# Edge attention on one core: score clipping and exponentials for two batches at a time, ScalarE's address reads behind its copies, norms one round later, 191 column tiles

## The chip, the cores and the metric

The kernel runs on one core of one Trainium2 chip. Its metric is device time in microseconds; the number that counts is the median of several executions. A profile is one further execution, recorded by the hardware profiler. Engines go by the profile's names: PE is TensorE (PEld its weight load), DVE VectorE, ACT ScalarE, POOL GpSimd, SP SyncE.

## The reference, cut to what matters

One graph attention layer with 6250 nodes and 206250 edges, 128 features in 8 heads of 16, edges sorted by destination:

```python
Qh, Kh, Vh = (h @ WQ), (h @ WK), (h @ WV)            # 6250 x 8 x 16 each
Eh = edge_attr @ WE                                   # 206250 x 8 x 16
score = einsum('ehd,ehd,ehd->eh', Kh[src], Qh[dst], Eh) / 4
score = exp(clip(score, -5, 5))
wV = segment_sum(Vh[src] * score[:, :, None], dst)
Z = segment_sum(score, dst)
out = layernorm(h + wV / (Z + 1e-6))
```

## The kernel before, in words

A **tile** is 128 edges (one per partition); there are 1612. A **batch** is four tiles (the last eight tiles go in smaller ones), 406 batches in all. `edge_attention` first writes a table of K and V rows to HBM, then runs one **round** per batch; the loop at L626 writes down the order of the instructions of every engine by hand. For a batch b the work is spread over three rounds:

- Round b (`stage_a`): PE multiplies the edge attributes by WE (`eps`, L498) and expands the destination's Q rows by a transposed one-hot (`qps`, L501).
- Round b+1 (`stage_b`): DVE multiplies K by Q (`kq`, L508), by the edge product (`kqe`, L511), sums over each head (`sc`, L514) and clips the scores to -20..20 (L517). At the round's end ACT (`weigh`) takes the exponential twice, into the message tile `msg` (L524) and into PSUM, `exp_p` (L525), a single buffer.
- Round b+2: DVE multiplies V by `exp_p` (`messages`, L558) and PE adds the batch into its window of 128 nodes with a one-hot (`stage_c`, `agg`, L578). One-hots are built for two batches at a time (`together`, L470 and L483), so every second round has two more DVE instructions.

K and V rows of a tile's sources reach SBUF in one of two ways. Most tiles are **gathered**: POOL issues one indirect DMA per tile (L430) from the table. POOL's queue holds little else, so it runs ahead of the rounds by as many batches as the 12 `kvrows` buffers and a manual dependency allow. One tile in some batches is a **column tile**: its sources' columns are copied out of the resident x by ACT (80 copies of one column, L403) and DVE (24 instructions that take two columns each, L400), PE multiplies the tile by the K and V weights (`colkv`, L412), and ACT puts the result into `kvrows` (L419). `COLP = (13, 6)` means six column tiles in 13 batches, 176 in all. The copies come in runs (ACT 10 runs of 8 a tile, DVE 6 runs of 4 instructions), spread over the rounds by `columns`. Before a run, the engine reads the run's column addresses from SBUF into registers (L392, one `TENSOR_LOAD` a run); `columns` reads for the next run before it issues the copies of this one. ACT's runs stand at two places of a round: behind the two exponentials, and at the start of the next round.

When all windows of two node blocks are there (24 times, about every 16 rounds), `finish` has PE add them up (`finps`, L537), ACT copies the result at the end of the round (`fin`, L551), and a layer norm of some 22 small DVE steps starts in the next round, first with `rz` (L791). `fill` issues one such step, or one of the Q rows that the next batches need, at each of four places in a round.

Of the kernel before, what the change touches and what calls it, by code (L numbers as in the profile page):

```python
# [9 lines left out]
F32 = mybir.dt.float32  # L10
# [17 lines left out]
MW = D + H  # L28
CH = 8
GB = 12  # L30
XB = 12
# [5 lines left out]
LAST = NT - TAIL  # L37
# [12 lines left out]
QLOOK = 3  # L50
QREG = 16
COL0 = 24
COLP = (13, 6)
COLA = (8, 10)
COLV = (8, 6)
COLL = 8
RING = 4096
XCOLS = 5
SUMS = 9
XT_AT = RING + P  # L60
NB = (N + P - 1) // P

# [40 lines left out]
def edge_attention(ctx: ExitStack, tc: tile.TileContext, x, xT, srcT, srcC, dstT, dstB, dst0, bnd, lo, eaT,  # L103
                   wq, wkv, we, out, kv, qtab, qs, relD):
    nc = tc.nc
# [35 lines left out]
    with ExitStack() as fast:  # L141
# [99 lines left out]
        wp = fast.enter_context(tc.tile_pool(name="work", bufs=3))  # L241
# [55 lines left out]
        xbs, stores, norms, pending, ready, finished, loaded_x = {}, [], [], [], [], [], set()  # L297
# [47 lines left out]
        chunks, aggs, sums, st8, expanded = {}, {}, {}, {}, {}  # L345

        def load_chunk(c):
            if c in chunks or c * CH >= NT:
# [21 lines left out]
        addresses, fetched = {}, {}  # L370

        def columns(eng, b, share=1.0, most=99):

            size, runs = COLA if eng is nc.scalar else COLV
            first = 0 if eng is nc.scalar else COLA[0] * COLA[1]
            engine = mybir.EngineType.Activation if eng is nc.scalar else mybir.EngineType.DVE
            copy = eng.copy if eng is nc.scalar else eng.tensor_copy
            due = int((b - COL0 + COLL - 1 + share) * runs * COLP[1] / COLP[0] + 1e-6)
            total = len(col_batches) * runs
            while copied.get(engine, 0) < min(due, total) and most:  # L380
                most -= 1
                k, j = divmod(copied.get(engine, 0), runs)
                copied[engine] = copied.get(engine, 0) + 1
                if k not in col_tiles:
                    col_tiles[k] = wp.tile([P, P], F32, name="xcol", bufs=XCOLS)
                to, j = col_tiles[k].bitcast(U8), first + j * size
                known = addresses.setdefault(engine, [])
                while len(known) < 2 and fetched.get(engine, 0) < total:
                    kf, jf = divmod(fetched.get(engine, 0), runs)
                    fetched[engine] = fetched.get(engine, 0) + 1  # L390
                    jf = first + jf * size
                    known.append(nc.values_load_multi_w_load_instructions(  # L392
                        col_at[kf % col_half:kf % col_half + 1, kf // col_half, jf:jf + size], engines=(engine,),
                        min_val=XT_AT, max_val=XT_AT + 8 * (N - 1) + 4,
                        skip_runtime_bounds_check_because="edges name nodes")[1])
                at = known.pop(0)
                if eng is nc.vector:
                    for c in range(0, size, 2):
                        both = [xT_bytes[:, ds(a - XT_AT, 8)] for a in at[c:c + 2]]
                        eng.tensor_tensor(to[:, 4 * (j + c):4 * (j + c) + 8], *both, op=ALU.bitwise_or)  # L400
                    continue
                for c in range(size):
                    copy(to[:, 4 * (j + c):4 * (j + c) + 4], xT_bytes[:, ds(at[c] - XT_AT, 4)])  # L403

        def project_columns(b):

# [47 lines left out]

        def together(b):

            t0 = batches[b][0]
            n = len(batches[b])
            if n == B and b + 1 < nbat and len(batches[b + 1]) == B and t0 % (2 * B) == 0:
                return [b, b + 1]  # L460
            return [] if n == B and t0 % (2 * B) else [b]

        def stage_0(b):
            group = together(b)
# [40 lines left out]
        def stage_b(b):  # L505
            n, g, oh, pq, pe = st8[b]
            t0 = wp.tile([P, B, D], F32, name="kq", bufs=2)
            nc.vector.tensor_tensor(t0[:, :n], g[:, :n, :D], pq[:, :n], op=ALU.mult)  # L508
# [4 lines left out]
            sc = wp.tile([P, B, H], F32, name="sc")  # L513
            nc.vector.tensor_reduce(sc[:, :n], t1[:, :n].rearrange("p b (h d) -> p b h d", h=H),  # L514
                                    axis=AX.X, op=ALU.add)
            yield
            nc.vector.tensor_scalar(sc[:, :n], sc[:, :n], -20.0, 20.0, op0=ALU.max, op1=ALU.min)  # L517
            st8[b] = [n, g, oh, sc]

        def weigh(b):  # L520

            n, g, oh, sc = st8[b]
            m = wp.tile([P, B, MW], F32, name="msg")
            nc.scalar.activation(m[:, :n, D:], sc[:, :n], AF.Exp, scale=0.25)  # L524
            nc.scalar.activation(exp_p[:, :n], sc[:, :n], AF.Exp, scale=0.25)  # L525
            st8[b] = [n, g, oh, m]

        def windows(q):

# [24 lines left out]
            blocks_out.append(copied_out)  # L554

        def messages(b):
            n, g, oh, m = st8[b]
            nc.vector.tensor_tensor(  # L558
                m[:, :n, :D].rearrange("p b (h d) -> p b h d", h=H),
                g[:, :n, D:].rearrange("p b (h d) -> p b h d", h=H),  # L560
                exp_p[:, :n, :, None].to_broadcast([P, n, H, DH]), op=ALU.mult)

        def stage_c(b):
            n, g, oh, m = st8.pop(b)
            for i in range(n):
                t = batches[b][i]
                k, _ = window_of(t)
                q = t * N // NT // P
                if q % 2 == 0 and q < NB and q not in loaded_x:
                    loaded_x.add(q)  # L570
                    xbs[q] = load_x(nc, sp, x, q, min(2, NB - q))
                final = k == NT
                if k not in aggs:
                    aggs[k] = psA.tile([P, 1, MW], F32, name="agg")
                    if final:
                        add_windows(aggs[k][:, 0], QL, True, False)
                tail = t == NT - 1 or window_of(t + 1)[0] != k
                nc.tensor.matmul(aggs[k][:, 0], oh[0][:, oh[1] + i * P:oh[1] + i * P + P], m[:, i, :],  # L578
                                 start=not final and t % (QUAD * G) == 0, stop=tail)
                if tail and final:  # L580
                    norms.insert(0, layernorm(nc, sp, aggs.pop(k), xbs.pop(QL), out, QL, 1, stores))
                elif tail:
                    sums[k] = sp.tile([P, MW], F32, name="sum", bufs=SUMS)
                    nc.scalar.copy(sums[k], aggs.pop(k)[:, 0])
# [40 lines left out]
        held, late = [], []  # L625
        for b in range(nbat + 3):  # L626
            if b >= XB and not manual:
                manual.append(fast.enter_context(tc.manual_schedule()))
# [4 lines left out]
            if b < nbat:  # L633
# [3 lines left out]
                g = gathered.pop(b)  # L637
# [221 lines left out]
```

## Time and profile before

| | |
|---|---|
| median of 3 runs | 1847.12 us (1847.1 to 1848.22) |
| profiled execution, its own time | 1840.47 us |
| its span | 1838.7 us |
| mean granted TensorE clock | 0.931 |
| PE / DVE / ACT / POOL busy | 71% / 94% / 87% / 75% |
| gathers issued by POOL | 1436 |
| clips, exponentials | 406, 812 |

The profile lists groups of instructions with their count, busy time and mean duration, then the time that the engine stood idle before them and what ended it. Small instructions overlap at their ends, so the start of the next one, in the timeline, tells better than the duration what one costs its engine. "issue" as the reason for a wait means that nothing in the profile held the engine: it was its own sequencer, for instance while it read addresses into registers (shown as ACTq and DVEq).

### The profile page before, as it was taken

To read this page: it belongs to the slowest core of one execution; us is meant where nothing else is said; L and a number is where in the kernel's file an instruction comes from. 1 tells how busy PE (TensorE), PEld (TensorE's weight loads), DVE (VectorE), ACT (ScalarE), POOL (GpSimd) and SP (SyncE) were. 2 spreads that over 40 slices of the span, in tenths; PEclk is the share of its full clock that TensorE was granted. 3 is DMA by queue.
4 is the path that set the end of the run, shared out by engine and by line. 5 is a ranking of instruction groups with operands and counts; after the bars stand their busy time and mean duration, and the time that the engine had idled before them with its cause. 6 is when DMAs were issued, how large, how long until landed. Compare 5 with 4: busy or idle time off the path is not lost.

```text
span 1838.7 us, 48927 instructions
## 1 busy us (share of the span) xinstructions
PE 1299.2 (71%) x9130; PEld 1118.7 (61%) x9130; DVE 1720.6 (94%) x7478; ACT 1608.3 (87%) x15268; POOL 1375.8 (75%) x1443
## 2 busy tenths in 40 slices
PE   6886667676676777776777667766767667766776
PEld 4776656565665666665666556655656656655665
DVE  5579999999999999999999999999999999999998
ACT  2339889899999999999999999999999999999994
POOL 6777777777777777777777777777777777777774
PEclk8999899889989899999899999999999999899989
DMA  8776667676776577677667766866876676667762
GB/s 281 231 228 199 192 183 225 194 205 196 211 221 202 177 224 216 182 208 221 202 199 213 226 192 183 241 198 180 241 213 191 192 229 194 203 185 232 217 191 77
DMA packets 170631, 376.74 MB, mean 205 GB/s; under 512 B 58423, under 2 KB 84369, under 8 KB 170315
## 3 DMA queue, kind: packets, MB, share of 16 engines
q0 software_dynamic: 68144, 185.10, 35.0%
q1 hardware_dynamic: 101031, 187.38, 33.9%
q14 instruction: 242, 1.98, 0.3%
q8 instruction: 74, 1.21, 0.3%
q10 hardware_dynamic: 1140, 1.06, 0.2%
HBM read 358.60 MB, written 14.81 MB: 203 GB/s over the span
## 4 chain that ended last, share of the span: by engine, by line
DVE 42%; DMA 17%; ACT 13%; PE 11%; issue 6%; DVEq 5%; POOL 4%; ACTq 2%; SPq 0%; POOLq 0%
DMA kvrows<-kv,src 14%; ACT xcol L403 11%; DVE xcol L400 8%; DVE kqe L511 6%; DVE kq L508 6%; DVE sc L514 6%; POOL kvrows L430 4%; DVEq L392 4%; DVE onehot L470 4%; PE eps L498 4%; DVE msg L558 4%; PE agg L578 3%; DVE onehotT L483 2%; ACTq L392 2%; DMA dB_sb<-dstB 1%
## 5 line engine op out<-in xcount | busy, mean ns | idle before, releaser
L430 POOL DMA_INDIRECT kvrows<-kv,src x1388 | 1328.6, 957 | 423.0 <-issue 313.0
L403 ACT COPY xcol<-xT_sb 128x4 uint8 x14080 | 1422.3, 191 | 60.5 <-issue 54.2
L498 PE MATMUL eps<-we_sb,ea 128*128 128x128 f32 x3224 | 488.9, 298 | 384.8 <-issue 182.7
L498 PEld LDWEIGHTS eps<-we_sb,ea 128*128 128x128 f32 x3224 | 425.0, 205 | 482.6 <-issue 353.7
L578 PE MATMUL agg<-msg,onehot 128*128 128x136 f32 x3224 | 526.0, 310 | 109.4 <-DVE msg L558 101.1
L578 PEld LDWEIGHTS agg<-msg,onehot 128*128 128x128 f32 x3224 | 447.0, 208 | 165.6 <-DVE msg L558 152.2
L400 DVE TENSOR_TENSOR xcol<-xT_sb 128x8 uint8 x4224 | 416.1, 156 | 8.7 <-issue 4.6
L508 DVE TENSOR_TENSOR kq<-kvrows,qps 128x512 f32<-128x512 f32 x406 | 274.0, 675 | 35.2 <-PE qps L501 17.1
L558 DVE TENSOR_TENSOR msg<-kvrows,exp_p 128x512 f32<-128x512 f32 x406 | 271.1, 668 | 7.5 <-ACT exp_p L525 7.5
L511 DVE TENSOR_TENSOR kqe<-kq,eps 128x512 f32<-128x512 f32 x406 | 272.3, 671 | 3.1 <-PE eps L498 2.6
L514 DVE TENSOR_REDUCE sc<-kqe 128x32 f32<-128x512 f32 x406 | 270.2, 665 | 0.5
L501 PE MATMUL qps<-qw,onehotT 126*128 126x128 bf16 x1612 | 166.6, 227 | 0.0
L524 ACT ACTIVATE msg<-sc 128x32 f32<-128x32 f32 x406 | 92.6, 228 | 72.0 <-DVE sc L517 64.5
L470 DVE TENSOR_TENSOR onehot<-iota_p,dst_sb 128x512 f32<-128x512 f32 (+2 forms) x206 | 137.5, 668 | 2.0 <-PE agg L578 2.0
L501 PEld LDWEIGHTS <-onehotT 126*128 126x128 bf16 x1612 | 132.9, 102 | 8.2
L412 PE MATMUL colkv<-wkv_sb,xcol 128*128 128x256 f32 x352 | 114.2, 409 | 0.8 <-ACT xcol L403 0.8
L483 DVE TENSOR_SCALAR onehotT<-relb,node 126x1024 bf16<-126x1024 bf16 (+2 forms) x206 | 100.0, 486 | 3.3 <-DMA relb<-relD 2.0
L517 DVE TENSOR_SCALAR sc<-sc 128x32 f32<-128x32 f32 x406 | 82.1, 202 | 0.3
L525 ACT ACTIVATE exp_p<-sc 128x32 f32<-128x32 f32 x406 | 73.7, 182 | 0.0
L419 ACT COPY kvrows<-colkv 128x256 f32<-128x256 f32 x176 | 63.8, 362 | 0.3 <-PE colkv L412 0.3
L430 POOL DMA_INDIRECT kvrows<-x,src x48 | 46.3, 964 | 22.5 <-issue 11.6
L412 PEld LDWEIGHTS colkv<-wkv_sb,xcol 128*128 128x128 f32 x352 | 59.7, 209 | 1.0 <-ACT xcol L403 1.0
(76 smaller groups left out, 537.3 us busy)
## 6 DMA issues: line engine op xcount, KB each, us to landing
ea<-eaT SPq DMA_DIRECT2D x201, 512.0 KB
relb<-relD SPq DMA_DIRECT2D x100, 504.0 KB
kvrows<-kv,src POOLq DMA_INDIRECT x1388
qw<-qs SPq DMA_DIRECT2D x202, 31.5 KB
kv<-kvst SPq DMA_DIRECT2D x12, 512.0 KB
qs<-qst SPq DMA_DIRECT2D x48, 96.0 KB
xst<-xT SPq DMA_DIRECT2D x12, 256.0 KB
xb<-x SPq DMA_DIRECT2D x24, 128.0 KB
```

The source lines that it names most:

```text
L400: eng.tensor_tensor(to[:, 4 * (j + c):4 * (j + c) + 8], *both, op=ALU.bitwise_or)
L403: copy(to[:, 4 * (j + c):4 * (j + c) + 4], xT_bytes[:, ds(at[c] - XT_AT, 4)])
L412: nc.tensor.matmul(pk, col_tiles.pop(k), wkv_sb, start=True, stop=True)
L430: ins = nc.gpsimd.indirect_dma_start(out=g[:k, i, :f], out_offset=None, in_=rows, in_offset=bass.IndirectOffsetOnAxis(ap=src_col(t)[:k], a ...
L470: nc.vector.tensor_tensor(tl[:, HW:].rearrange("p (t n) -> p t n", n=P)[:, :n, :HW], iota_p[:, None, :].to_broadcast([P, n, HW]), rel[:, t ...
L498: nc.tensor.matmul(pe[:, i, :], ea[:, i * P:i * P + P], we_sb, start=True, stop=True)
L501: expanded[b] = nc.tensor.matmul(pq[:, i, :], ohT[:, i * P:i * P + P], loaded[t0 // WT], start=True, stop=True)
L508: nc.vector.tensor_tensor(t0[:, :n], g[:, :n, :D], pq[:, :n], op=ALU.mult)
L511: nc.vector.tensor_tensor(t1[:, :n], t0[:, :n], pe[:, :n], op=ALU.mult)
L514: nc.vector.tensor_reduce(sc[:, :n], t1[:, :n].rearrange("p b (h d) -> p b h d", h=H), axis=AX.X, op=ALU.add)
L558: nc.vector.tensor_tensor(m[:, :n, :D].rearrange("p b (h d) -> p b h d", h=H), g[:, :n, D:].rearrange("p b (h d) -> p b h d", h=H), exp_p[ ...
L578: nc.tensor.matmul(aggs[k][:, 0], oh[0][:, oh[1] + i * P:oh[1] + i * P + P], m[:, i, :], start=not final and t % (QUAD * G) == 0, stop=tail)
```

## The change

Four edits, and sizes that follow from them:

- **Pairs.** Batches 12 to 399 are clipped and weighed in pairs (2i, 2i+1). Both write their head sums into one tile `sc` of eight tiles' width; behind the second one DVE clips all 64 columns at once, and ACT takes the two exponentials of 64 columns at once. `sc`, `msg` and `exp_p` are twice as wide; `sc` and `msg` have two buffers, not three. Messages and aggregation of both batches move one round later, to b+3, one batch in each round as before. Batches 0 to 11 and from 400 on go alone, at their old places. `kvrows` of a paired batch is held one round longer, with the same 12 buffers.
- **Address reads.** ACT reads the addresses of its next run behind the copies of a run, one run ahead. DVE's reads stay in front, two runs ahead.
- **Norms.** A layer norm starts one round later (`waiting`), but not in the last rounds.
- **Column tiles.** `COLP` is (2, 1): one column tile in every two batches, 191 in all, so 15 more, with 15 fewer gathers. `XCOLS` goes from 5 to 4 buffers of a column tile, `SUMS` from 9 to 8.
- `together` now also pairs the small last batches, which makes two one-hot builds fewer there.

```diff
-COLP = (13, 6)
+COLP = (2, 1)
-XCOLS = 5
-SUMS = 9
+XCOLS = 4
+SUMS = 8
...
-        exp_p = psX.tile([P, B, H], F32, name="exp_p")
+        exp_p = psX.tile([P, 2 * B, H], F32, name="exp_p")
...
-                while len(known) < 2 and fetched.get(engine, 0) < total:
...
+                fetch(2 if eng is nc.vector else 1)
                 at = known.pop(0)
...
                     copy(to[:, 4 * (j + c):4 * (j + c) + 4], xT_bytes[:, ds(at[c] - XT_AT, 4)])
+                fetch(1)
...
+        def group_of(b):
+
+            if b < XB or b >= LAST // B - 1:
+                return [b]
+            return [b - b % 2, b - b % 2 + 1]
+
+        def weighed(r):
+
+            return [b for b in (r - 3, r - 2) if 0 <= b < nbat and b + (3 if len(group_of(b)) > 1 else 2) == r]
...
-            nc.vector.tensor_scalar(sc[:, :n], sc[:, :n], -20.0, 20.0, op0=ALU.max, op1=ALU.min)
-            st8[b] = [n, g, oh, sc]
+            if b == group[-1]:
+                nc.vector.tensor_scalar(sc[:, :k + n], sc[:, :k + n], -20.0, 20.0, op0=ALU.max, op1=ALU.min)
...
-            n, g, oh, sc = st8[b]
-            m = wp.tile([P, B, MW], F32, name="msg")
+            group = group_of(b)
+            if b != group[-1]:
+                return
+            sc, n = scores.pop(group[0]), sum(len(batches[i]) for i in group)
+            m = wp.tile([P, 2 * B, MW], F32, name="msg", bufs=2)
...
-            norms.extend(pending)
+            norms.extend(waiting)
+            waiting[:] = pending
             pending.clear()
+            if b >= nbat - 3:
+                norms.extend(waiting)
+                waiting.clear()
...
-            if 0 <= b - 2 < nbat:
-                messages(b - 2)
+            for i in weighed(b):
+                messages(i)
...
-            if 0 <= b - 2 < nbat:
-                stage_c(b - 2)
+            for i in weighed(b):
+                stage_c(i)
```

How this moves instructions. First ACT, in the middle of the program, where a round's exponentials stand (`xcol` is the column tile being filled, `col_at` the table of addresses, `kvrows<-colkv` the finished column tile's copy). Before:

```order
L403 COPY xcol<-xT_sb 128x4 x8
L419 COPY kvrows<-colkv 128x256
L524 ACTIVATE msg<-sc 128x4x8
L525 ACTIVATE exp_p<-sc 128x32
L392 TENSOR_LOAD col_at
L403 COPY xcol<-xT_sb 128x4 x8
L392 TENSOR_LOAD col_at
```

After, at the end of a pair's second round:

```order
L407 COPY xcol<-xT_sb 128x4 x8
L394 TENSOR_LOAD col_at
L545 ACTIVATE msg<-sc 128x8x8
L546 ACTIVATE exp_p<-sc 128x64
L407 COPY xcol<-xT_sb 128x4 x8
L394 TENSOR_LOAD col_at
```

The read that stood between the exponentials and the next run of copies now stands ahead of the exponentials, behind the run before; between two runs there is one read as before. The next pair of exponentials comes two rounds later, with ten runs between.

Second DVE, from the head sums of one round to the `kqe` product of the next, in the middle of the program. Before (here with no step of a norm):

```order
L514 TENSOR_REDUCE sc<-kqe 128x32
L558 TENSOR_TENSOR msg<-kvrows,exp_p 128x4x128
L392 TENSOR_LOAD col_at
L400 TENSOR_TENSOR xcol<-xT_sb 128x8 x4
L517 TENSOR_SCALAR sc<-sc 128x32
L508 TENSOR_TENSOR kq<-kvrows,qps 128x512
L392 TENSOR_LOAD col_at
L400 TENSOR_TENSOR xcol<-xT_sb 128x8 x4
L511 TENSOR_TENSOR kqe<-kq,eps 128x512
```

After, at the end of a pair's second round; the next round here starts a norm (`rz`):

```order
L531 TENSOR_REDUCE sc<-kqe 128x32
L580 TENSOR_TENSOR msg<-kvrows,exp_p 128x4x128
L394 TENSOR_LOAD col_at
L404 TENSOR_TENSOR xcol<-xT_sb 128x8 x4
L536 TENSOR_SCALAR sc<-sc 128x64
L522 TENSOR_TENSOR kq<-kvrows,qps 128x512
L394 TENSOR_LOAD col_at
L404 TENSOR_TENSOR xcol<-xT_sb 128x8 x4
L817 TENSOR_SCALAR rz<-fin 128x16
L525 TENSOR_TENSOR kqe<-kq,eps 128x512
```

The clip is there in every second round only, at twice the width, and a norm's first step keeps its place in a round but comes a round after the one that copies `fin`. In the whole program DVE has 212 clips for 406, and ACT 1910 runs of copies for 1760.

More of the change, by code (lines that the diff above doesn't have):

```diff
@@ L343, in load_rel @@
                               .to_broadcast([QROWS, n]))
-        chunks, aggs, sums, st8, expanded = {}, {}, {}, {}, {}
+        chunks, aggs, sums, st8, expanded, scores = {}, {}, {}, {}, {}, {}
         def load_chunk(c):
@@ L387, in columns, with fetch @@
                 known = addresses.setdefault(engine, [])
-                while len(known) < 2 and fetched.get(engine, 0) < total:
[L389 to L395, printed above, removed]
+                def fetch(ahead):
+                    while len(known) < ahead and fetched.get(engine, 0) < total:
+                        kf, jf = divmod(fetched.get(engine, 0), runs)
+                        fetched[engine] = fetched.get(engine, 0) + 1
+                        jf = first + jf * size
+                        known.append(nc.values_load_multi_w_load_instructions(
+                            col_at[kf % col_half:kf % col_half + 1, kf // col_half, jf:jf + size],
+                            engines=(engine,), min_val=XT_AT, max_val=XT_AT + 8 * (N - 1) + 4,
+                            skip_runtime_bounds_check_because="edges name nodes")[1])
+                fetch(2 if eng is nc.vector else 1)
                 at = known.pop(0)
@@ L455, in together @@
         def together(b):
[L457 to L461, printed above, removed]
+            first = LAST // B
+            if (b - first if b >= first else b) % 2:
+                return []
+            return [i for i in (b, b + 1) if i < nbat and (i < first) == (b < first)]
+        def group_of(b):
[4 more added lines that the diff above has]
+            return [b for b in (r - 3, r - 2) if 0 <= b < nbat and b + (3 if len(group_of(b)) > 1 else 2) == r]
         def stage_0(b):
@@ L512, in stage_b @@
             yield
[L513 to L514 removed]
+            group = group_of(b)
+            if b == group[0]:
+                scores[b] = wp.tile([P, 2 * B, H], F32, name="sc", bufs=2)
+            sc, k = scores[group[0]], sum(len(batches[i]) for i in group if i < b)
+            nc.vector.tensor_reduce(sc[:, k:k + n], t1[:, :n].rearrange("p b (h d) -> p b h d", h=H),
                                     axis=AX.X, op=ALU.add)
+            st8[b] = [n, g, oh, k]
             yield
[L517 to L518 removed]
+            if b == group[-1]:
+                nc.vector.tensor_scalar(sc[:, :k + n], sc[:, :k + n], -20.0, 20.0, op0=ALU.max, op1=ALU.min)
         def weigh(b):
[L522 to L523 removed]
+            group = group_of(b)
+            if b != group[-1]:
+                return
+            sc, n = scores.pop(group[0]), sum(len(batches[i]) for i in group)
+            m = wp.tile([P, 2 * B, MW], F32, name="msg", bufs=2)
             nc.scalar.activation(m[:, :n, D:], sc[:, :n], AF.Exp, scale=0.25)
             nc.scalar.activation(exp_p[:, :n], sc[:, :n], AF.Exp, scale=0.25)
[L526 removed]
+            for i in group:
+                st8[i].append(m)
         def windows(q):
@@ L623, in fill @@
                 norms.pop(0)
-        held, late = [], []
+        held, late, waiting = [], [], []
         for b in range(nbat + 3):
```

10 lines of the change are left out of this document (5 added, 5 removed).

## The prediction

> **What bounds the kernel now.** The page first: how busy the engines are, and whether that changes over the span.
>
> ```profile
> span 1838.7 us, 48927 instructions
> ...
> PE 1299.2 (71%) x9130; PEld 1118.7 (61%) x9130; DVE 1720.6 (94%) x7478; ACT 1608.3 (87%) x15268; POOL 1375.8 (75%) x1443
> ...
> DVE  5579999999999999999999999999999999999998
> ACT  2339889899999999999999999999999999999994
> POOL 6777777777777777777777777777777777777774
> ```
>
> After two slices of preparation nothing changes: DVE and ACT above 0.8 or 0.9, POOL flat at 0.7. A flat 0.7 is suspicious, so the second view is POOL's own waits.
>
> ```profile
> POOL kvrows L430 <- issue: 324.6, 1065, 0.3
> ...
> POOL kvrows L430 <- PE kvacc L279: 7.2, 3, 6.0
> ```
>
> POOL's longest wait for its sequencer is 0.3 us, 1065 times, and nothing else holds it except in the preparation. A gather is 0.96 us plus a fixed gap of 0.30: POOL issues without a break, and its 75% is full. So I compare paces. The same 400 us in two window tables, gathers (L430) first, then `kq` (L508), one a batch:
>
> ```profile
> 500.00:900.00 400.00, 303.09 (x319) 0.92 0.70 205
> ```
>
> ```profile
> 500.00:900.00 400.00, 61.77 (x92) 0.92 0.70 205
> ```
>
> POOL: 400/319 = 1.254 us a gather, and a batch has 4 - 6/13 = 3.54 of them: **4.44 us a batch**. DVE: 400/92 = **4.35**. POOL began far ahead and DVE gains 0.09 us a batch on it; who waits in the end is in DVE's waits:
>
> ```profile
> DVE kq L508 <- PE qps L501: 17.1, 29, 1.0
> DVE rz L791 <- ACT fin L551: 15.7, 16, 2.5
> ...
> DVE msg L558 <- ACT exp_p L525: 7.5, 10, 1.3
> ...
> DVE kq L508 <- DMA kvrows<-kv,src: 6.5, 6, 1.8
> ```
>
> Only 6.5 us in six waits are for gathered rows, all behind 1377 us. DVE thus sets the pace to about 1400 us and POOL barely the rest: the two limits lie within 7 us of each other. ACT is the third:
>
> ```profile
> ACT msg L524 <- DVE sc L517: 64.5, 75, 4.5
> ACT xcol L403 <- issue: 54.2, 188, 1.2
> ...
> ACT fin L551 <- PE finps L537: 12.3, 10, 2.4
> ```
>
> In 331 of 406 rounds ACT reaches the exponentials after the clip is done, without waiting. It has 131 us of slack in all, 7%.
>
> **The change, part by part.** I sum along DVE, from one batch to the next, against the profiled execution's own 1840.47 us (span 1838.7 and 1.8 around it). The median of the runs shown is 6.65 above that, and I add the difference to it.
>
> *Column tiles, DVE.* The timeline of DVE:
>
> ```profile
> 908.94 0.38 DVE L400 TENSOR_TENSOR xcol<-xT_sb 128x8 uint8 x4
> 909.25 0.14 DVE L809 SCALAR_TENSOR_TENSOR y<-w,y 128x2 f32<-128x2 f32 x1
> 909.32 0.28 DVE L517 TENSOR_SCALAR sc<-sc 128x32 f32<-128x32 f32 x1
> 909.43 0.18 DVE L807 TENSOR_TENSOR w<-y 128x2 f32<-128x2 f32 x1
> ```
>
> A run of four instructions takes 0.31 us from its start to the next one's. 15 tiles x 6 runs x 0.31 = **+27.9 us**. DVE has no idle time to hide them in.
>
> *Column tiles, POOL.* 15 gathers x 1.254 = 18.8 us less issue, and 4.39 us a batch. DVE keeps its distance longer, so its 6.5 us of waits for rows should go: **-6.5**, and no more, since POOL was not the limit before that.
>
> *Clips.* 406 become 212. One costs 0.11 us above (909.32 to 909.43), and 0.08 in front of a large one:
>
> ```profile
> 1792.54 0.17 DVE L517 TENSOR_SCALAR sc<-sc 128x32 f32<-128x32 f32 x1
> 1792.62 0.68 DVE L508 TENSOR_TENSOR kq<-kvrows,qps 128x512 f32<-128x512 f32 x1
> ...
> 1795.03 0.67 DVE L558 TENSOR_TENSOR msg<-kvrows,exp_p 128x512 f32<-128x512 f32 x1
> ```
>
> Width costs little: 8 to 16 columns is 3 ns by the rows of the last batches.
>
> ```profile
> L517 DVE TENSOR_SCALAR sc<-sc 128x16 f32<-128x16 f32 x3 | 0.5, 167 | 0.0
> ...
> L517 DVE TENSOR_SCALAR sc<-sc 128x8 f32<-128x8 f32 x2 | 0.3, 164 | 0.0
> ```
>
> The wide clip is not in the trace; I take 0.02 us more (3 ns x 4 gives 0.01; a second clip's 0.11 is the other end). 194 x (0.09 - 0.02) = **-13.6 us**, between 0 and -19.
>
> *Norms.* `rz` stands second in DVE's queue behind `kq`, with `kqe`, the sums and the messages behind it, and it waits until ACT has copied `fin`, which waits for 16 matmuls. A round later the copy is long there: up to -15.7. But those matmuls also delay PE's next `eps` and `qps`, and what is late next is `kq`. The timeline has the longest but one:
>
> ```profile
> 537.23 3.23 PE L537 MATMUL finps<-sum,shift 128*128 128x136 f32 x16
> ...
> 540.91 0.17 DVE L791 TENSOR_SCALAR rz<-fin 128x16 f32<-128x16 f32 x1 [2.33 <-ACT fin L551]
> ```
>
> With `finps` at 3.23 us, PE comes to the next `eps` that much later, and I expect half of such a wait to return. I take **-11**, between -4 and -15.7.
>
> *ACT.* It gets 15 x 80 more copies, 15 more `kvrows` copies, half the exponentials, and loses the 0.3 us gaps where a read stood bare.
>
> ```profile
> 906.17 4.11 ACT L403 COPY xcol<-xT_sb 128x4 uint8 x40 [0.32 <-issue]
> 910.19 0.23 ACT L524 ACTIVATE msg<-sc 128x32 f32<-128x32 f32 x1
> 910.32 0.18 ACT L525 ACTIVATE exp_p<-sc 128x32 f32<-128x32 f32 x1
> 910.44 3.66 ACT L403 COPY xcol<-xT_sb 128x4 uint8 x37
> ```
>
> Two exponentials take 0.25 us (910.19 to 910.44), the pair's perhaps 0.30. 40 copies take 4.02 us (906.17 to 910.19), 37 start within 3.66: 80 copies are 7.7 to 8.0 us. Two rows more:
>
> ```profile
> 901.13 0.36 ACT L419 COPY kvrows<-colkv 128x256 f32<-128x256 f32 x1
> 901.39 0.23 ACT L524 ACTIVATE msg<-sc 128x32 f32<-128x32 f32 x1
> ```
>
> The `kvrows` copy is 0.26. Sums and `fin` follow from their groups:
>
> ```profile
> L584 ACT COPY sum<-agg 128x136 f32<-128x136 f32 x101 | 26.6, 263 | 4.2 <-PE agg L578 4.0
> ...
> L551 ACT COPY fin<-finps 128x272 f32<-128x272 f32 x24 | 9.2, 384 | 12.6 <-PE finps L537 12.3
> ```
>
> (26.6 + 9.2)/203 pairs is 0.18, less their overlap some 0.13. So ACT needs **8.4 to 8.7 us for a pair**, about 8.55. DVE's pair is 2 x 4.35 = 8.70 now, and after the terms above (1/13 tile x 1.86 = +0.14, clip -0.07, norm -0.06) 8.71. ACT ends up within 2% of DVE. On average it fits, but not pair by pair: a norm adds its 22 steps to about six rounds, and pairs without one are shorter than 8.7. There ACT falls behind. How far it may: from the clip's start to the messages are 2.49 us (1792.54 to 1795.03), of which clip and exponentials take about 0.5; so 2 us, and beyond that `msg` waits on `exp_p`, with `kq` and all else of DVE behind it. I charge **+5 us**, between 0 and +20.
>
> The address read itself:
>
> ```profile
> L392 ACTq TENSOR_LOAD <-col_at x1760: 537/557/1479, 131.5 to 1806.7; - x196
> ```
>
> 0.56 us lie behind eight copies of 0.1. The 40 copies in 4.02 us and the 37 in 3.66 differ by 0.004 us a copy, so some reads are not wholly covered; that is why I take a middle value. The Trainium skill (Advanced Engine Details and Errata, Engine Queue Depths) gives ScalarE a queue of eight instructions, which would cover eight copies' worth, more than 0.56, in every run. By that rule the pair comes to 8.4 and the +5 to about 0; by the 40 copies to 8.7 and to the upper end.
>
> *At nothing.* The 15 `colkv` matmul pairs (PE idles 29%; bare they would be 0.6 us each, 9 in all). The 90 more address reads of DVE, covered by the 1.3 us of reduction and messages ahead (bare 0.6 each). Fewer buffers of `xcol` and `sum`: a column tile is multiplied four rounds after its last copy, and a window is read before its buffer comes round. `kvrows` held a round longer: POOL may run one batch less ahead, 4.4 us, and it loses its lead so slowly now that DVE does not see it. Two fewer one-hots in the tail: at most -0.8.
>
> Sum: 27.9 - 6.5 - 13.6 - 11 + 5 = **+1.8 us, 1842.3 of its own time, 1849 as a median**. The gathers saved are worth 19 us to POOL, but nearly all of it is time that DVE spends on copying columns.
>
> **The rivals.**
>
> 1. *POOL's gain shows.* The looser order takes out most of DVE's waits (`rz`, `msg`, and part of `qps`: 30 to 40 us of 47), and ACT is never late. Then DVE does a pair in 8.6, and the end follows POOL's, which comes 18.8 earlier: -5 to -17, 1830 to 1842. For it: DVE's waits are real and all in rounds that the change loosens. Against: `qps` hangs on PE, which is untouched.
> 2. *ACT becomes the bound.* With 8.7 a pair and `fin`'s 12.3 us of stalls (0.06 a pair), it exceeds DVE's 8.71 from about 8.65 on; `msg` then waits for `exp_p` in most pairs: 0.05 to 0.1 over 190 pairs, on top of +1.8 less the 5: +6 to +16, 1853 to 1863. For it: the 40 copies in 4.02. Against: its stalls shrink when it is late anyway.
> 3. *The norm's wait only moves* to `kq` behind `qps`: +11 more, 1860. Against it: most of the 16 waits are under 1 us, and PE idles.
> 4. *DVE as the one bound.* If only DVE's work counts, columns less clips are +14: 1861. The Trainium skill (Perfetto Trace Analysis, Identifying the Most-Contended Engine) holds that the engine with the highest occupancy is the one to relieve, here DVE at 94%; by it the relief of POOL at 75% is worth nothing. The trace agrees for the first 1400 us, and not for the last 400, where the six waits for rows lie.
>
> **How the numbers follow.** Forecast (-4 to +8, 1843 to 1855): 0.42. Rival 1: 0.28. Rival 2: 0.20. Rivals 3 and 4: 0.05 each. The range leaves out the far end of rival 1 and the last of rival 2: 1834 to 1862. 0.2% of the median is 3.7 us, about what a measurement of this kernel can tell from no change. Faster: rival 1 and 0.04 of the forecast, 0.32. Within: 0.26 of the forecast and 0.01 of the slow ones, 0.27. Slower: 0.41.
>
> **What would show it.** Right: DVE busy up by some 14 us; no waits of `kq` on gathered rows and none of `rz`; ACT near 93%, its waits for issue nearly gone and for the clip fewer; POOL done some 15 us or more before the end with rows waiting; some waits of `msg` on `exp_p` in pairs without a norm. Those waits above 15 us would be rival 2; `kq` on `qps` above 25 us, rival 3; `kq` still waiting for rows with a shorter span, rival 1. Wrong throughout would be a new wait that I have not named, such as gathers held by buffers.

## The result: level, and the profile after

| | before | after |
|---|---|---|
| median (22 executions each, same chip) | 1847.11 us | **1846.78 us** |
| ratio, 95% interval | | 0.9998 [0.9991, 1.0005] |
| profiled execution, its own time | 1840.47 us | 1845.89 us |
| its span | 1838.7 us | 1844.0 us |
| mean granted TensorE clock | 0.931 | 0.923 |

By the medians nothing changed. The two profiled executions differ by 5.4 us, because the one of before lay 6.6 us under its median and the one of after 0.9 us. So the terms are compared from the traces, and the sums from the medians. Of the executions reported below, one of the change without columns (3760.76 us, unexplained) and three of the last group are slow; the ratios leave them out, the medians given do not. First the page of after, engines' busy time:

```profile
span 1844.0 us, 50160 instructions
...
PE 1307.6 (71%) x9160; PEld 1129.0 (61%) x9160; DVE 1731.1 (94%) x7640; ACT 1658.1 (90%) x16095; POOL 1363.4 (74%) x1428
```

DVE has 10.5 us more to do and is still at 94%; POOL has 12.4 us less; ACT went from 87% to 90%. DVE's waits of after (engine and tile, what it waited for, total us, times, longest):

```profile
DVE kq L522 <- PE qps L515: 29.2, 31, 5.0
...
DVE msg L580 <- ACT exp_p L546: 9.0, 11, 1.5
...
DVE kq L522 <- DMA kvrows<-kv,src: 2.5, 2, 1.9
...
DVE rz L817 <- ACT fin L573: 1.9, 1, 1.9
```

The waits for `rz` went from 15.7 to 1.9 us and those for gathered rows from 6.5 to 2.5, while `kq` behind `qps` grew from 17.1 to 29.2 and `msg` from 7.5 to 9.0. These four sum to 4.2 us less. DVE's whole idle time (span less busy time) fell by 5.2 us, so the four hold most of that, and with 10.5 us more work they give +6.3 where the spans differ by 5.3. (That busy and idle time make up the span is so for every engine; what this sum shows is only which waits changed.)

ACT's waits of after:

```profile
ACT msg L545 <- DVE sc L536: 74.0, 71, 7.5
...
ACT fin L573 <- PE finps L559: 8.4, 5, 3.7
...
ACT xcol L407 <- issue: 2.9, 11, 0.6
```

The waits for issue between runs of copies fell from 54.2 us in 188 to 2.9 in 11, which is what ACT gained from reading behind its copies. The same 400 us stretches of after as in the window tables of before, first the gathers (L435):

```profile
500.00:900.00 400.00, 303.41 (x318) 0.95 0.70 207
900.00:1300.00 400.00, 303.41 (x318) 0.94 0.70 207
1300.00:1700.00 400.00, 300.28 (x313) 0.93 0.69 204
```

And `kq` (L522), one a batch:

```profile
500.00:900.00 400.00, 62.45 (x92) 0.95 0.70 207
...
1300.00:1700.00 400.00, 62.41 (x92) 0.93 0.69 204
```

DVE does 92 batches in 400 us, as before. POOL issues 313 instead of 318 gathers in the last stretch: it is now held back, because it stays ahead. POOL's own waits say so:

```profile
POOL kvrows L435 <- issue: 322.8, 1043, 2.1
POOL kvrows L435 <- PE qps L515: 21.1, 41, 4.6
```

And the second of these two lines as it was before:

```profile
POOL kvrows L430 <- PE qps L501: 9.8, 32, 0.3
```

Most of the 41 waits are still the fixed gap of 0.3, but the longest is 4.6: these are gathers that the manual dependency does not let run further ahead. Before, no wait outside the preparation was longer than the fixed gap. Behind the preparation, 15 gathers of after wait 0.5 us or more, 17.4 us beyond the gap. Seven of them (7.4 us, between 255 and 435 us) are of another kind: each starts some 0.74 us behind the end of a `messages` instruction, as a wait for a buffer of `kvrows` would look, and a paired batch keeps that one round longer. It costs nothing here, since POOL is far enough ahead again at 1528 us for the dependency to hold it. At the end of the span the timeline of after has one thing that is not in the trace of before:

```profile
1807.97 2.37 ACT L407 COPY xcol<-xT_sb 128x4 uint8 x24
...
1810.39 1.22 PE L417 MATMUL colkv<-wkv_sb,xcol 128*128 128x256 f32 x2 [5.03 <-ACT xcol L407]
...
1813.78 0.69 DVE L522 TENSOR_TENSOR kq<-kvrows,qps 128x512 f32<-128x512 f32 x1 [5.02 <-PE qps L515]
1814.02 0.94 POOL L435 DMA_INDIRECT kvrows<-kv,src  x1 [4.64 <-PE qps L515]
```

In the brackets: ACT finishes its last column tile late, PE's next instruction waits 5.03 us for it, and `qps`, `kq` and a gather stand behind PE. That is 5.0 of the 12.1 us by which `kq` behind `qps` grew.

### The profile page after: what moved, and what is told of

It reads as the page before. It is cut to its first block, busy times and chain, and to the rows that moved or that the text cites. A ratio compares the mean times of both kernels' runs of the same rounds, so it can differ in the third digit from the quotient of the medians.

```text
span 1844.0 us, 50160 instructions
## 1 busy us (share of the span) xinstructions
PE 1307.6 (71%) x9160; PEld 1129.0 (61%) x9160; DVE 1731.1 (94%) x7640; ACT 1658.1 (90%) x16095; POOL 1363.4 (74%) x1428
## 4 chain that ended last, share of the span: by engine, by line
DVE 41%; PE 19%; ACT 9%; DMA 8%; issue 8%; DVEq 4%; POOL 3%; ACTq 1%; SPq 0%; POOLq 0%
PE agg L600 8%; DVE xcol L404 8%; ACT xcol L407 8%; DMA kvrows<-kv,src 7%; PE eps L512 7%; DVE kqe L525 7%; DVE kq L522 7%; DVE sc L531 5%; DVE msg L580 5%; DVEq L394 4%; DVE onehot L484 3%; POOL kvrows L435 3%; DVE onehotT L497 2%; PE colkv L417 2%; PE qps L515 1%
## 5 line engine op out<-in xcount | busy, mean ns | idle before, releaser
L435 POOL DMA_INDIRECT kvrows<-kv,src x1373 | 1316.8, 959 | 435.9 <-issue 310.1
L407 ACT COPY xcol<-xT_sb 128x4 uint8 x15280 | 1507.6, 192 | 4.4 <-issue 2.9
L404 DVE TENSOR_TENSOR xcol<-xT_sb 128x8 uint8 x4584 | 454.3, 158 | 9.4 <-issue 5.1
L522 DVE TENSOR_TENSOR kq<-kvrows,qps 128x512 f32<-128x512 f32 x406 | 274.2, 675 | 42.3 <-PE qps L515 29.2
L484 DVE TENSOR_TENSOR onehot<-iota_p,dst_sb 128x512 f32<-128x512 f32 (+1 forms) x204 | 137.5, 675 | 0.9 <-PE agg L600 0.9
L417 PE MATMUL colkv<-wkv_sb,xcol 128*128 128x256 f32 x382 | 132.0, 431 | 5.2 <-ACT xcol L407 5.0
L545 ACT ACTIVATE msg<-sc 128x64 f32<-128x64 f32 (+2 forms) x212 | 53.7, 254 | 80.3 <-DVE sc L536 74.0
L497 DVE TENSOR_SCALAR onehotT<-relb,node 126x1024 bf16<-126x1024 bf16 (+1 forms) x204 | 100.4, 492 | 5.3 <-DMA relb<-relD 3.9
L417 PEld LDWEIGHTS colkv<-wkv_sb,xcol 128*128 128x128 f32 x382 | 69.0, 221 | 5.6 <-ACT xcol L407 5.6
L435 POOL DMA_INDIRECT kvrows<-x,src x48 | 45.7, 951 | 22.7 <-issue 12.8
L559 PE MATMUL finps<-sum,shift 128*128 128x136 f32 x370 | 49.4, 287 | 0.0
L536 DVE TENSOR_SCALAR sc<-sc 128x64 f32<-128x64 f32 (+2 forms) x212 | 47.0, 222 | 0.3
```

The source lines that it names most:

```text
L417: nc.tensor.matmul(pk, col_tiles.pop(k), wkv_sb, start=True, stop=True)
L435: ins = nc.gpsimd.indirect_dma_start(out=g[:k, i, :f], out_offset=None, in_=rows, in_offset=bass.IndirectOffsetOnAxis(ap=src_col(t)[:k], a ...
L484: nc.vector.tensor_tensor(tl[:, HW:].rearrange("p (t n) -> p t n", n=P)[:, :n, :HW], iota_p[:, None, :].to_broadcast([P, n, HW]), rel[:, t ...
```

## Experiments

**Theory** (from the prediction and the two traces): there are two limits of nearly one height. One is POOL's 1436 gathers, issued without a break; the other is DVE's queue, with ACT feeding it. The columns relieve POOL and load DVE; pairs, reads and norms relieve DVE; together they cancel. **Rivals**: each edit is worth little anyway (the norm's wait moves to `qps`; reads and pairs are covered), or ACT is what decides. Every kernel was run beside the kernel before on the same chip.

### One edit at a time, on the kernel before

Columns alone:

```diff
-COLP = (13, 6)
+COLP = (2, 1)
```

> The kernel before with COLP (2, 1) alone: 15 more column tiles, no pairs, old reads, old norms. Theory (DVE's queue sets the pace, POOL is a second limit 6.5 us behind it): DVE gets 27.9 us of copies and loses its 6.5 us of waits for gathered rows, so +21 us against before, and kq never waits for rows. Rival 1 (POOL is the limit): 15 gathers less, -10 us or better. Rival 2 (ACT is the limit, with two exponentials a batch and bare reads: 8.9 us for two batches against 8.7): +30 us or more, with msg waiting for exp_p in most batches.

Measured: 1892.51 us against 1842.91, ratio 1.0270 [1.0251, 1.0289], +49.6: over twice the theory's figure, and in the rival's range. DVE's waits of this kernel:

```profile
DVE kq L508 <- PE qps L501: 28.7, 40, 4.9
DVE rz L791 <- ACT fin L551: 26.6, 21, 2.4
...
DVE msg L558 <- ACT exp_p L525: 8.9, 11, 1.3
```

ACT is late here, but not where the rival (and the prediction) looked for it. `msg` hardly waits more than before (8.9 for 7.5). `rz` does, 26.6 for 15.7, since the copy of `fin` stands behind ACT's late copies; and the last column tile is late by 4.9 us. Work +27.9 (DVE's busy time in the trace rose by 30.0), `rz` +10.9, `qps` +11.6, `msg` +1.4 and rows -4.8 (1.7 are left) make 47, and the profiled executions differ by 44.3. In the old order a column tile costs DVE its copies and about two thirds as much again in waits. POOL is far from a limit here; it is held for long:

```profile
POOL kvrows L430 <- PE qps L501: 53.5, 57, 7.6
```

Pairs alone (the change with columns, reads and norms undone; the smaller `XCOLS` and `SUMS` and the pairing of the last one-hots stay):

```diff
-COLP = (2, 1)
+COLP = (13, 6)
-                fetch(2 if eng is nc.vector else 1)
+                while len(known) < 2 and fetched.get(engine, 0) < total:
...
-            norms.extend(waiting)
-            waiting[:] = pending
+            norms.extend(pending)
...
```

> The changed kernel with COLP back at (13, 6), reads in front of the copies and norms in the old round: pairs alone. Theory (DVE sets the pace, POOL second): DVE loses 13.6 us of clips, but POOL's 1436 gathers are still there, so the gain stops where DVE meets POOL: -2 to -6 us. Rival 1 (POOL is the limit): 0. Rival 2 (ACT is the limit): half of its exponentials go, 39 us, so -6 us too, but with ACT's waits for the clip down.

Measured: 1848.64 us, ratio 1.0025 [1.0011, 1.0040], +5.7. The sign was wrong. The windows of `kq` (L518) in this kernel, and two of DVE's waits:

```profile
500.00:900.00 400.00, 63.18 (x93) 0.95 0.70 208
900.00:1300.00 400.00, 61.61 (x91) 0.94 0.70 205
1300.00:1700.00 400.00, 61.03 (x90) 0.92 0.69 202
```

```profile
DVE rz L809 <- ACT fin L569: 21.6, 23, 2.4
DVE kq L518 <- DMA kvrows<-kv,src: 20.0, 18, 3.0
```

DVE is faster at first (93 for 92), uses up POOL's lead, and from then on goes at POOL's pace: 400/90 is 4.44 us, which is 3.54 gathers of 1.254. Waits for rows are 20.0 us where they were 6.5, and those of `rz` 21.6 where they were 15.7; DVE's busy time is 12.1 us less. What the clips save, DVE spends waiting. That alone would give 0, the figure of rival 1. The span of this trace is 8.5 us longer than that of before, in two parts: the last gather starts 4.6 us later, and from there to the end it takes 3.9 us more. A part of the first is that gathers are held: four between 240 and 370 us wait 7.1 us beyond the gap, which none did before, and the two long ones start behind a `messages`, for instance:

```profile
340.01 0.68 DVE L576 TENSOR_TENSOR msg<-kvrows,exp_p 128x512 f32<-128x512 f32 x1
```

```profile
341.44 0.94 POOL L431 DMA_INDIRECT kvrows<-kv,src  x1 [3.43 <-PE eps L508]
```

That looks like the `kvrows` buffer again. How much of the 4.6 us it makes is open: with the reads or the norms alone no gather is held for long, and the last one starts 3.0 us later than before as well.

Reads alone (ACT's reads behind its copies):

```diff
+                fetch(2 if eng is nc.vector else 1)
...
+                fetch(1)
```

> The kernel before with ACT's address reads behind a run's copies, alone. Theory (ACT is not on the path): ACT's 54 us of waits for issue become waits for the clip, and the time moves by less than 1.5 us. Rival 2 (ACT is a limit): -5 us or better.

Measured: 1844.43 us, ratio 1.0005 [0.9994, 1.0016]. That is +1.5, within the noise. As the theory has it, ACT's waits for issue (3.7 us are left) became waits for the clip, 123.2 us where they were 64.5.

Norms alone:

```diff
-            norms.extend(pending)
+            norms.extend(waiting)
+            waiting[:] = pending
...
```

> The kernel before with norms one round later, alone. Theory: rz's 15.7 us of waits go, up to half of the long ones return as kq waiting for qps, and POOL's queue caps the gain: -2 to -6 us. Rival 3 (the wait only moves): kq's waits for qps grow from 17 to some 30 us and the time stays within 1.5 us.

Measured: 1844.59 us, ratio 1.0007 [0.9997, 1.0018]. That is +1.7, next to the rival's figure and no gain, but not by the rival's cause. The windows of `kq` (L508) and the waits:

```profile
500.00:900.00 400.00, 63.45 (x94) 0.96 0.71 208
900.00:1300.00 400.00, 61.09 (x90) 0.91 0.69 202
1300.00:1700.00 400.00, 61.39 (x90) 0.91 0.69 204
```

```profile
DVE kq L508 <- DMA kvrows<-kv,src: 28.6, 18, 3.3
DVE kq L508 <- PE qps L501: 19.4, 36, 1.6
```

`qps` took over only 2.3 us of the 15.7; the norms did speed DVE up, to 94 batches in the first stretch, and the gathered rows took the rest, 28.6 us for 6.5. It is POOL's limit again.

### The change with one edit undone

Without the columns:

```diff
-COLP = (2, 1)
+COLP = (13, 6)
```

> The changed kernel with COLP back at (13, 6): pairs, reads and norms together, 1436 gathers. Theory now (two limits of one height, POOL's 1436 gathers and DVE's queue; relief of one alone shows nothing): POOL issues without a break and ends where it did, kq waits for gathered rows from about batch 150 on, 20 us or more in all, and the time is 0 to +5 us against before, as with pairs alone. Rival (DVE is the one limit): the 13.6 us of clips and 11 of norms come out, -20 us or better.

Measured: 1846.01 us against 1845.22, ratio 1.0002 [0.9989, 1.0016]. Within the expectation. Windows of `kq` (L522), and its waits for gathered rows:

```profile
500.00:900.00 400.00, 63.59 (x94) 0.94 0.71 209
900.00:1300.00 400.00, 61.16 (x90) 0.91 0.69 203
1300.00:1700.00 400.00, 60.57 (x89) 0.91 0.69 202
```

```profile
DVE kq L522 <- DMA kvrows<-kv,src: 27.7, 21, 3.4
```

Pairs, reads and norms together are still worth nothing while POOL has 1436 gathers to issue. They free DVE up to 94 batches, and then POOL sets 90 or less. The waits for rows are 27.7 us, where the theory said 20 or more, and nearly all lie behind 920 us. In six more waits `kq` stands 10.3 us for which the profile names no releaser.

With the reads in front again:

```diff
-                fetch(2 if eng is nc.vector else 1)
+                while len(known) < 2 and fetched.get(engine, 0) < total:
...
-                fetch(1)
```

> The changed kernel with ACT's reads in front of the copies again. Theory (with 191 column tiles ACT has 2% to spare, and what it loses in bare reads comes out as late fin copies and exponentials): ACT's waits for issue return, 30 to 50 us, and the time is +4 to +12 us against before. Rival (reads are worth nothing, as when moved alone): within 2 us of before.

Measured: 1851.99 us, ratio 1.0036 [1.0020, 1.0053], +6.8, as the theory had it; the waits for issue, 25.7 us, came out a little under its 30 to 50. ACT's and DVE's waits of this kernel:

```profile
ACT msg L541 <- DVE sc L532: 42.2, 30, 7.2
ACT xcol L404 <- issue: 25.7, 101, 1.1
```

```profile
DVE msg L576 <- ACT exp_p L542: 13.7, 23, 1.4
```

22.8 us more of issue on ACT cost it 32 us of its slack at the clip, and DVE 4.7 us more at `msg`. `kq` behind `qps` gives some of it back (22.9 for 29.2), and DVE's busy time is 2.8 us more; these two traces differ by 6.3 us.

With norms at once:

```diff
-            norms.extend(waiting)
-            waiting[:] = pending
+            norms.extend(pending)
...
```

> The changed kernel with norms in the old round. Theory (DVE is the limit here, since POOL was relieved): rz waits 20 us or more for ACT's fin copy, and all but what kq then waits less for qps comes out: +6 to +15 us against before. Rival (the wait only moves between rz and kq): within 2 us of before.

Measured: 1860.69 us, ratio 1.0086 [1.0064, 1.0108], +15.5, just past the upper end of the theory's range.

```profile
DVE rz L813 <- ACT fin L573: 25.8, 23, 2.2
DVE kq L522 <- PE qps L515: 14.5, 17, 5.0
```

The same edit that is worth nothing on the kernel before is worth 15 us on the changed one, since there DVE and not POOL is the limit. Also: `rz` and `qps` exchange with each other. Where `rz` waits 25.8, `qps` waits 14.5; in the changed kernel 1.9 and 29.2.

### The end of the span

In the changed kernel the last column tiles come late. The last four (batches 397 to 400) as gathers:

```diff
-    n = (last - 2 - COL0 + COLL) * COLP[1] // COLP[0]
+    n = (last - 2 - COL0 + COLL) * COLP[1] // COLP[0] - 4
```

> The changed kernel with the last four column tiles (batches 397 to 400, bunched there) gathered: 187 column tiles, the last in batch 396. Theory (PE stood 5.0 us at the end for the last column tile's copies, and DVE behind it): that wait is gone, DVE has 7.4 us of copies less, and POOL has its 4 gathers (5 us) free there: -4 to -9 us against before. Rival (POOL is the limit at the end): 0.

Measured: 1844.74 us, ratio 0.9994 [0.9979, 1.0010]: the rival's case. DVE's waits:

```profile
DVE kq L522 <- PE qps L515: 18.5, 28, 2.5
...
DVE kq L522 <- DMA kvrows<-kv,src: 14.9, 14, 2.2
```

PE's 5 us wait for the column tile is gone (the longest behind `qps` is 2.5), but the waits for rows rose by 12.4. Three of them are those of the last full batches, 398 to 400, by the timeline:

```profile
1801.95 0.69 DVE L522 TENSOR_TENSOR kq<-kvrows,qps 128x512 f32<-128x512 f32 x1 [2.18 <-DMA kvrows<-kv,src]
1806.45 0.69 DVE L522 TENSOR_TENSOR kq<-kvrows,qps 128x512 f32<-128x512 f32 x1 [1.43 <-DMA kvrows<-kv,src]
1811.43 0.69 DVE L522 TENSOR_TENSOR kq<-kvrows,qps 128x512 f32<-128x512 f32 x1 [1.95 <-DMA kvrows<-kv,src]
```

These make 5.6 us, about what the column tile cost: the last batches now have four gathers each, 4 x 1.254 = 5.0 us, more than DVE's 4.35. Most of the other waits for rows lie before 1750 us, where both kernels still give the same instructions, so they belong to this execution and not to the edit. The two limits meet at the end as well.

### The last group: another chip

These four kernels ran on another chip, on which the kernel before took 2498.7 us (granted clock in the profiled executions of the four: 0.757 to 0.764). So they say little of the level of the other runs, and the changed kernel itself has no run there. Three of them try to mend the end: one column tile less (`- 1` in the line above); pairs up to batch 397 only; both, and no norm held in the last five rounds. The fourth is the change without pairs. All four expectations were missed.

```diff
-    n = (last - 2 - COL0 + COLL) * COLP[1] // COLP[0]
+    n = (last - 2 - COL0 + COLL) * COLP[1] // COLP[0] - 1
```

> The changed kernel with one column tile less (190): the last one's copies are then due two rounds ahead of its matmul, not in the same round. Theory (PE's 5.0 us at the end wait for the last tile's copies, which have no round to spare): that wait is gone, the rest as it was: -3 to -6 us against before. Rival (POOL or the tail behind sets the end anyway, as when four were dropped): within 2 us of before.

Measured: 2555.45 us, 1.0182 [1.0135, 1.0229].

```diff
-            if b < XB or b >= LAST // B - 1:
+            if b < XB or b >= LAST // B - 3:
```

> The changed kernel with pairs up to batch 397, so that batches 398 to 400 go alone and the last finish comes one round earlier; all else, the wait for the last column tile too, as changed. Theory (pairs lengthen the tail by 2 to 3 us, since the last windows are summed a round later): -2 to -3 us against before. Rival (the wait for the last column tile covers it): within 1 us of before.

Measured: 2574.06 us, 1.0280 [1.0242, 1.0317].

```diff
-    n = (last - 2 - COL0 + COLL) * COLP[1] // COLP[0]
+    n = (last - 2 - COL0 + COLL) * COLP[1] // COLP[0] - 1
...
-            if b < XB or b >= LAST // B - 1:
+            if b < XB or b >= LAST // B - 3:
...
-            if b >= nbat - 3:
+            if b >= nbat - 5:
```

> The changed kernel with both mended: 190 column tiles, pairs up to batch 397, and norms not held back in the last five rounds. Theory (the loop is level with before and the change loses its gain in the tail): -5 to -9 us against before, faster than both kernels. Rival (POOL's queue sets the end): within 3 us of before.

Measured: 2546.68 us, 1.0199 [1.0173, 1.0226].

```diff
...
-            if b == group[-1]:
-                nc.vector.tensor_scalar(sc[:, :k + n], sc[:, :k + n], -20.0, 20.0, op0=ALU.max, op1=ALU.min)
+            nc.vector.tensor_scalar(sc[:, :n], sc[:, :n], -20.0, 20.0, op0=ALU.max, op1=ALU.min)
...
```

(The tiles' widths and buffers, the exponentials, the place of the messages and the pairing of the last one-hots go back with it.)

> The changed kernel without pairs: columns, reads and norms as changed, clips and exponentials for each batch, messages two rounds behind, old one-hots at the end. Theory (columns are paid for with what the other three edits free on DVE and ACT): DVE has 13.6 us of clips more, ACT 40 us of exponentials, the tail is some 3 us shorter: +10 to +25 us against before, with msg waiting for exp_p more often. Rival (pairs alone made the kernel slower, so the rest is better without them): below before, -3 us or better.

Measured: 2550.28 us, 1.0211 [1.0180, 1.0241]. The waits of ACT and of DVE in this one:

```profile
ACT xcol L406 <- issue: 488.4, 881, 1.2
```

```profile
DVE msg L562 <- ACT exp_p L529: 406.7, 266, 5.6
```

In this kernel, on that chip, ACT is the limit: it stands 488 us for its own sequencer between copies, in pieces of up to 1.2 us, and DVE stands 407 us for the exponentials. What all four share against the kernel before are the new place of the reads, 14 or 15 more column tiles, and, but for rounds at the end, the later norms. That it is the column tiles' copies on ACT that make them 2 to 3% slower is likely from these waits, but no run there separates it, and the kernel before has no trace there. `no_pairs` is no slower than `one_less_col`, which has pairs; so nothing about the pairs, nor about the end of the span, follows from these runs for the level that the prediction is about. What the pairs are worth in company stays open there too. A version that beats both kernels was thus not found, and whether mending the end gives one stays open.

## Why the prediction was right

1849 was forecast and 1846.78 came, with the reason that was given: "The gathers saved are worth 19 us to POOL, but nearly all of it is time that DVE spends on copying columns." The trade of one limit for the other is borne out by the runs. That the figure came so close is in part luck. By the prediction's terms DVE's work rises by 14 us and its waits fall by 12.5 (-6.5, -11 and +5); between the traces its busy time rose by 10.5 and its idle time fell by 5.2. The two errors go against each other, and the traces then differ by +5.4 where +1.8 was forecast, while the medians differ by -0.3. Point by point:

- **Two limits close to each other: shown**, and they are closer than I used. Pairs, norms, reads, and all three together, each left the time where it was or above, and the columns alone cost 49.6 us. The prediction summed the terms as if each counted by itself (-13.6 for the clips, -11 for the norms). The norms and the reads count only together with the gathers that the columns take off POOL (undone there they cost 15.5 and 6.8 us); for the pairs this was not measured at this level. The expectations for pairs and norms alone fell on that: I read POOL's 0.09 us a batch as a limit that starts at 1400 us, and not as one that gives back at once whatever DVE gains. The start of the last gather says it in one column:

| kernel | gathers | last gather starts | span | from there to the end |
|---|---|---|---|---|
| before | 1436 | 1821.04 | 1838.7 | 17.7 |
| reads alone | 1436 | 1824.05 | 1842.9 | 18.9 |
| norms alone | 1436 | 1824.05 | 1844.0 | 20.0 |
| pairs alone | 1436 | 1825.63 | 1847.2 | 21.6 |
| change without columns | 1436 | 1822.11 | 1843.1 | 21.0 |
| after | 1421 | 1821.80 | 1844.0 | 22.2 |
| columns alone | 1421 | 1863.34 | 1883.0 | 19.7 |

With 1436 gathers the last one starts between 1821 and 1826, whatever DVE was spared. With 1421 it is not POOL's pace that sets it: after, it waits 1.35 us for `qps`.

- **Columns +27.9 on DVE: the size holds.** The eight runs of four between 899 and 909 us in the timeline of after take 0.30 to 0.37 us to the start of what follows, against the 0.31 that was taken. DVE's busy time rose by 10.5 us, where 14 were named. The waits that follow a late ACT (`rz`, the last column tile) were not in the term; columns alone brought them out.
- **Rows -6.5: about so**, 6.5 to 2.5. The last gather of batch 400 ends 9.9 us ahead of the batch's `kq`, where it was 2.1. The sign that I named for it, POOL done 15 us or more before the end, was none: it is 22.2 now, but was 17.7 before.
- **Clips -13.6: the step holds.** The timeline of after, a wide clip ahead of `kq`:

```profile
1804.34 0.18 DVE L536 TENSOR_SCALAR sc<-sc 128x64 f32<-128x64 f32 x1
1804.44 0.67 DVE L522 TENSOR_TENSOR kq<-kvrows,qps 128x512 f32<-128x512 f32 x1
```

0.10 from start to start, where the narrow one had 0.08: the 0.02 that was taken.

- **Norms -11: the mechanism holds, the return was larger than half.** `rz` gave 13.8 us, and `kq` behind `qps` took 12.1, of which 5.0 are the late column tile and not the norms: 7.1 of 13.8 came back, or -6.7 in these two waits. That all 7.1 come from the norms is inferred: with the norms alone `qps` took over only 2.3. Undone in the changed kernel, the edit costs some 15 us. Its trace is 11.7 us longer than that of after, at the same busy time of DVE, and the two waits make 9.2 of that; the rest is in small waits of several kinds. The median lies further off because that profiled execution was 3.1 us under its median, and the one of after 0.9.
- **ACT +5: hardly any of it in the steady rounds.** A pair with no wait in it, from the timeline of after:

```profile
901.40 0.25 ACT L545 ACTIVATE msg<-sc 128x64 f32<-128x64 f32 x1
901.55 0.20 ACT L546 ACTIVATE exp_p<-sc 128x64 f32<-128x64 f32 x1
901.70 2.37 ACT L407 COPY xcol<-xT_sb 128x4 uint8 x24
...
909.93 0.26 ACT L545 ACTIVATE msg<-sc 128x64 f32<-128x64 f32 x1
```

8.53 us from pair to pair, and 0.30 for the two exponentials, as estimated. But over the span ACT still has 74.0 us at the clip, and `msg` waits only 1.5 us more than before. By the rule of the Trainium skill (Advanced Engine Details and Errata, Engine Queue Depths; eight instructions for ScalarE), eight copies of 0.1 cover a read of 0.56: the 2.9 us of issue that are left agree with it. So rival 2 fell. What ACT's fuller time did cost are the 5.0 us of the last column tile, which the prediction put at nothing ("a column tile is multiplied four rounds after its last copy"): at the end that isn't so. That this is also 5 is chance; the term was meant for `msg` behind `exp_p`.
- **`kvrows` held a round longer, put at nothing: by the look of the trace it does hold gathers**, for 7.4 us in the changed kernel and for most of 7.1 us with pairs alone. The prediction named gathers held by buffers as a sign of being wrong throughout. It was none: in the changed kernel POOL has 15 gathers fewer and makes the time up.
- **Not named either**: pairs hold the last batches one round longer. From the last gather to the end, pairs alone need 3.9 us more than before, norms alone 2.3. This was not priced; that the longer staging is the cause was argued and not tested at this level.
- **Rival 1** (POOL's gain shows) would have needed DVE's waits to go; those on `qps` grew instead. **Rival 3** was to be seen by more than 25 us of `kq` on `qps`, and 29.2 came; but 5.0 are the late tile, and with the norms at once the kernel is slower by 15 us, so the wait did not merely move. **Rival 4**: the Trainium skill (Perfetto Trace Analysis, Identifying the Most-Contended Engine) would relieve the engine with the highest occupancy. Pairs and norms alone relieve DVE, at 94%, and bring nothing: here the trace goes against it, since POOL at 75% was issuing without a break, and this rival's 1861 did not come.

Of the 5 us at the end and the 4 us of the pairs' tail one could think that they hide a real gain. Gathering the last four column tiles gave the first and lost it to POOL; the second was not settled.

## What to carry to other kernels

Where two engines limit at one height, an experiment with one edit at a time shows nothing for each, and the edit that trades one engine for the other shows a loss; take single edits back out of the whole as well before calling them useless (the norms: 0 alone, 15 us in company). An engine with a fixed gap between its instructions can be full at 75% busy: look at its longest wait, not at its share. And look at the last few microseconds of such a change on their own, as late side work is paid there (5.0 us for the last column tile here) and deeper staging may be.

## What the runs showed of the hardware

- An address read of 0.56 us that stands between the exponentials and a run of copies left 54.2 us of issue waits (188 of them); behind a run of eight copies it left 2.9 (11 of them).
- Clips and exponentials of these small tiles cost little more at twice the width: it made the clip 0.10 us instead of 0.08, and both exponentials together 0.30 instead of 0.25.
- On the chip of the last group ACT's copies took as long as ever (190 ns each by the profile, 192 in the changed kernel) and yet it stood 488.4 us for its own sequencer. What held that sequencer is not known.
